# Layer 0 of a four-layer graph network: upper score blocks only, the adjacency used without a turn

## The chip, the cores and the metric

One core of one Trainium2 chip runs the whole program. The metric is the device time of one execution in microseconds (us). Engines are named as in the profile: PE is TensorE (matrix products and transposes), PEld its weight loads, DVE is VectorE, ACT is ScalarE, POOL is GpSimd, and SP is the engine that issues most DMAs.

## The reference, cut to what matters

There are 16 graphs ("batches") of 1024 nodes with 128 features. Layer 0 is a graph attention, and the change lies in it and in how its adjacency reaches layer 1.

```
h = x @ W_w.T + W_b
e = einsum('bjl,bkl->bjk', h @ A, h);  e = e + swapaxes(e, 1, 2)      # symmetric
att = where(adj > 0, e, -9e15);  att = softmax(att, axis=1) * adj
h_prime = relu(einsum('bij,bjk->bik', att, h))
coeff = sigmoid(concatenate([x, h_prime]) @ gate_w.T + gate_b)
x = layernorm(x + coeff * x + (1 - coeff) * h_prime)
```

The inputs are built as `adj = a | a.T | eye`, so each adjacency is symmetric, holds 0 and 1, and has a full diagonal. Layer 1 first thins the adjacency row by row ("dilation"), then runs three neighbour averages with weights and norms. Layer 2 is another attention and layer 3 a small graph convolution.

## The kernel before, in words

The program is one Python function `fast_kernel`. It also computes a flag from several arrays, among them `other`, `bad`, `past` and `nomem`; where the flag is set, a second function, `general_kernel`, recomputes everything. `other` is filled in layer 0 and is non-zero where an adjacency entry is neither 0 nor 1.

A batch's rows are handled in 8 tiles of 128. Layer 0 has three generators. `before(s, b)` loads the eight adjacency row tiles `an` (fp32, 512 KB each, two buffers), and for each one: ACT copies it to bf16 `ab` and sums the rows to `deg` (L922); DVE compares it with its own 0/1 form into `chk` and counts differences in `other` (L925); PE turns its eight blocks into the PSUM tile `pt` (L929); DVE writes them as fp8 columns of `Y[b]` (L930). In between, for tiles 1, 3, 5 and 7, it also forms `xT`, `hT`, `G` (the product of `As0` = A + A.T with `hT`) and `hn` (L934 to L949). At its end POOL stores `Y[b]` to memory, to `adj8_d[b]` (L951), for layers 2 and 3.

`attention(s, b)` goes over eight tiles jt: ACT makes a mask `msk` from a row tile of `Y` (0 for an edge, -2^53 for none, L962); PE computes the 128x1024 scores `e` from `hT` and `G` in two halves of 512 columns (`wide_matmul`, L723; the fp32 product is shown as two matmul records per half); DVE adds mask and scores into `em` with the row maximum as a by-product (L965) and negates it (L967); ACT takes the exponential in place (L969); DVE forms the reciprocal of the sum and scales the rows of `hn` to `hs` (L971, L973); PE adds `hs` times `em` to `acc` (L976). `after(s, b)` applies gate, sum and layer norm, and POOL stores the result to `x1_d`.

`in_turn` runs `after(b-1)`, `attention(b)` and `before(b+1)` alternately, so that batches overlap; at the end `attention(15)` runs beside `after(14)` alone. A scheduler then fixes each engine's instruction order in advance; on the chip every engine works through its own list in that order. The PSUM pools are `ps_w` (two score tiles of two banks), `ps_a` (`acc`) and `ps_h` (two tiles of one bank, shared by `pt` and all the small products).

The fp8 adjacency of all 16 batches stays on chip after layer 0, as four tiles of four batches, `Yq[0]` to `Yq[3]` ("quarters", the tiles called `carry`). Dilation works on it in two groups of eight batches (`GB` = 8): for each of eight blocks k and each group g, `prepare` forms counts, `fixed_point` finds the thresholds and `removal` clears edges. The order of (k, g) is the list `steps`. The batches 0 to 7 are stored to `dil8_d` (`dil_d` in the profile) after their last removal (L1154), and their space becomes `wide_pool` of layer 1, which holds the fp32 pieces `a` and the reloaded `A8` tiles. Layer 1 begins with batch 8.

Of the kernel before, what the change touches and what calls it, by code (L numbers as in the profile page):

```python
# [22 lines left out]
P = 128  # L23
NEG = -9000000000000000.0
BIG = 2.0 ** 53
# [4 lines left out]
QB = 4  # L30
# [609 lines left out]
def fast_kernel(ctx: ExitStack, tc: tile.TileContext, t: dict, out: bass.AP, flag: bass.AP):  # L640

    nc = tc.nc
    B, N, D = t["x"].shape
    NT = N // P
    H2 = N // 512
    BT = B * NT

    consts = ctx.enter_context(tc.tile_pool(name="consts", bufs=1))
    dram = ctx.enter_context(tc.tile_pool(name="dram", bufs=1, space=DRAM))

    identf = consts.tile([P, P], F32, name="identf")
    make_identity(nc, identf)
    identb = consts.tile([P, P], BF16, name="identb")
# [8 lines left out]
    adj8_d = [dram.tile([P, NT, N // 4], F32, name=f"adj8_d{b}") for b in range(B)]  # L662
# [9 lines left out]
    deg = consts.tile([P, BT], F32, name="deg")  # L672
# [1 line left out]

    bad = consts.tile([P, 2, NT, B], BF16, name="bad")
    past = consts.tile([P, NT - 2, B], F32, name="past")
    other = consts.tile([P, BT], F32, name="other")

    mx0 = consts.tile([P, BT], F32, name="mx0")
    zeros = mx0  # L680
# [39 lines left out]
    def wide_matmul(psum, lhsT, rhs, tag="w"):  # L720
        p = psum.tile([P, N], F32, name="pmm", tag=tag)
        for h in range(H2):
            nc.tensor.matmul(p[:, h * 512:(h + 1) * 512], lhsT, rhs[:, h * 512:(h + 1) * 512],  # L723
                             start=True, stop=True)
        return p
# [151 lines left out]


    carry_ctx, carry2_ctx = ExitStack(), ExitStack()
    Yq = []  # L880
    for ctx_, side in ((carry2_ctx, "right"), (carry_ctx, "left")):
        pool = ctx_.enter_context(tc.tile_pool(name=f"carry_{side}", bufs=1, side=side))
        Yq += [pool.tile([P, QB, NT, N], FP8, name=f"carry{len(Yq) + i}") for i in range(B // QB // 2)]
    Y = [Yq[b // QB][:, b % QB] for b in range(B)]

# [3 lines left out]
    with ExitStack() as ph:  # L889

        early = ph.enter_context(tc.tile_pool(name="l0_early", bufs=1, reuse_waits="tile"))
        wts = ph.enter_context(tc.tile_pool(name="l0_w", bufs=1, reuse_waits="tile"))
        ps_w = ph.enter_context(tc.tile_pool(name="l0_pw", bufs=2, space=PSUM, reuse_waits="tile"))
        ps_a = ph.enter_context(tc.tile_pool(name="l0_pa", bufs=1, space=PSUM, reuse_waits="tile"))
        ps_h = ph.enter_context(tc.tile_pool(name="l0_ph", bufs=2, space=PSUM, reuse_waits="tile"))

        with tc.tile_pool(name="l0_raw", bufs=1) as raw:
            W0T = transposed(wts, ps_h, matrix(raw, t["L0_gnn_W_w"], "l0W"), "l0WT", "h")
            As0 = symmetric(wts, ps_h, matrix(raw, t["L0_gnn_A"], "l0A"), "l0As", "h")
        work = ph.enter_context(tc.tile_pool(name="l0_work", bufs=1, reuse_waits="tile"))  # L900
        small = ph.enter_context(tc.tile_pool(name="l0_small", bufs=2, reuse_waits="tile"))
        b0 = column(wts, t["L0_gnn_W_b"], "l0b")
        gw = wts.tile([P, 2, 32], F32, name="l0gw")
# [4 lines left out]
        gbh = wts.tile([P, 1], F32, name="l0gbh")  # L908
        nc.vector.tensor_scalar(gbh, gb, 0.5, None, op0=OP.mult)
        nbig = wts.tile([P, 1], F32, name="l0nbig")  # L910
        nc.vector.memset(nbig, -BIG)

        def before(s, b):

            s.xn = work.tile([P, NT, P], F32, name="xn", bufs=3)
            nc.sync.dma_start(s.xn, nat(t["x"][b]))
            for it in range(NT):
                c = b * NT + it
                an = early.tile([P, N], F32, name="an", bufs=2)
                nc.sync.dma_start(an, t["adj"][b][it * P:(it + 1) * P, :])  # L920
                ab = early.tile([P, N], BF16, name="ab", bufs=2)
                nc.scalar.activation(ab, an, AF.Copy, accum_out=deg[:, c:c + 1])  # L922

                chk = early.tile([P, N], FP8, name="chk")
                nc.vector.scalar_tensor_tensor(chk, an, 0.0, an, op0=OP.is_gt, op1=OP.not_equal,  # L925
                                               accum_out=other[:, c:c + 1], saturate=False)
                pt = ps_h.tile([P, NT, P], BF16, name="pt", tag="h")
                for jt in range(NT):
                    nc.tensor.transpose(pt[:, jt, :], ab[:, jt * P:(jt + 1) * P], identb)  # L929
                nc.vector.tensor_scalar(Y[b][:, :, it * P:(it + 1) * P], pt, 0.0, None, op0=OP.is_gt, saturate=False)  # L930
                if it == 1:
                    xT = early.tile([P, N], F32, name="xT")
                    for p, c, _ in turned(ps_h, s.xn):
                        nc.scalar.copy(xT[:, c], p)  # L934
                elif it == 3:
                    s.hT = work.tile([P, N], F32, name="hT", bufs=2)
                    for p, c in products(ps_h, (W0T, xT)):
                        nc.scalar.activation(s.hT[:, c], p, AF.Identity, bias=b0)
                    pz = gates(ps_h, early.tile([P, N], FP8, name="chk").bitcast(F32), (gw[:, 0, :], xT))
                    s.gx = small.tile([P, NT], F32, name="gx")  # L940
                    nc.vector.tensor_copy(s.gx.rearrange("p (q t) -> p q t", t=2), pz[:, :, :, 0])
                elif it == 5:
                    s.G = work.tile([P, N], F32, name="G", bufs=2)
                    for p, c in products(ps_h, (As0, s.hT)):
                        nc.scalar.copy(s.G[:, c], p)
                elif it == 7:
                    s.hn = work.tile([P, N], F32, name="hn")
                    for p, c, _ in turned(ps_h, s.hT):
                        nc.vector.tensor_copy(s.hn[:, c], p)  # L949
                yield  # L950
            nc.gpsimd.dma_start(adj8_d[b], Y[b].bitcast(F32))  # L951

        def attention(s, b):


            s.acc = ps_a.tile([P, N], F32, name="acc")
            for jt in range(NT):
                js = slice(jt * P, (jt + 1) * P)
                c = b * NT + jt
                mx = mx0[:, c:c + 1]  # L960
                msk = work.tile([P, N], BF16, name="msk", bufs=2)
                nc.scalar.activation(msk, Y[b][:, jt, :], AF.Identity, scale=BIG, bias=nbig)  # L962
                e = wide_matmul(ps_w, s.hT[:, js], s.G)
                em = work.tile([P, N], F32, name="em", bufs=2)
                nc.vector.tensor_tensor_reduce(em, e, msk, 1.0, -3.0e38, op0=OP.add, op1=OP.max, accum_out=mx)  # L965
                nmx = small.tile([P, 1], F32, name="nmx")
                nc.vector.tensor_scalar(nmx, mx, -1.0, None, op0=OP.mult)  # L967
                sm = small.tile([P, 1], F32, name="sm")
                nc.scalar.activation(em, em, AF.Exp, bias=nmx, accum_out=sm)  # L969
                rs = small.tile([P, 1], F32, name="rs")  # L970
                nc.vector.reciprocal(rs, sm)  # L971
                hs = small.tile([P, P], F32, name="hs")
                nc.vector.tensor_scalar(hs, s.hn[:, js], rs, None, op0=OP.mult)  # L973
                for h in range(H2):
                    c = slice(h * 512, (h + 1) * 512)
                    nc.tensor.matmul(s.acc[:, c], hs, em[:, c], start=(jt == 0), stop=(jt == NT - 1))  # L976
                yield

        def after(s, b):
# [21 lines left out]

        in_turn(before, attention, after)

# [8 lines left out]
    with ExitStack() as ph:  # L1012
        sb = ph.enter_context(tc.tile_pool(name="dl_sb", bufs=2, reuse_waits="tile"))
        small = ph.enter_context(tc.tile_pool(name="dl_small", bufs=3, reuse_waits="tile"))
# [150 lines left out]


        G2 = B // GB
        steps = [(Batch(), k, g) for k in range(NT) for g in range(G2)]
        for s in steps[:G2]:
            for _ in prepare(*s):  # L1170
                pass

        nc.vector.tensor_scalar(mx0, mx0, -1.0e15, None, op0=OP.is_lt)
        nc.vector.tensor_reduce(nomem, mx0, AX.X, OP.max)

        nc.vector.tensor_scalar(deg, deg, 1.0, 1.0, op0=OP.add, op1=OP.max)
# [1 line left out]
        pt = ps_s.tile([BT, P], F32, name="pt", tag="s")  # L1178
# [74 lines left out]
    with ExitStack() as ph:  # L1253
        wts = ph.enter_context(tc.tile_pool(name="l1_w", bufs=1, reuse_waits="tile"))
        work = ph.enter_context(tc.tile_pool(name="l1_work", bufs=2, reuse_waits="tile"))
# [3 lines left out]
        small = ph.enter_context(tc.tile_pool(name="l1_small", bufs=2, reuse_waits="tile"))  # L1259
        ps_h = ph.enter_context(tc.tile_pool(name="l1_ph", bufs=4, space=PSUM, reuse_waits="tile"))  # L1260
# [185 lines left out]
        left = []  # L1446
# [4 lines left out]
        for l in range(3):  # L1451
# [9 lines left out]
            for i in range(B + lag[l]):  # L1461
                streams, left = left, []
# [22 lines left out]
            left = [rest]  # L1485
# [263 lines left out]
```

## Time and profile before

| what | value |
|---|---|
| time, median of 3 runs | 3006.41 us (3003.87, 3006.41, 3013.27) |
| profiled execution, first to last instruction | 2999.4 us |
| what lies around the span, against the median | 7.0 us |
| layer 0 (to the last norm of batch 15) | about 0 to 731 us |
| dilation | about 731 to 1146 us |
| layer 1 | about 1146 to 1820 us |
| layers 2 and 3 | the rest |
| PE busy, share of the span | 2738.3 us, 91% |
| DVE busy | 2327.9 us, 78% |
| ACT busy | 2028.5 us, 68% |

The page lists no time of its own for the profiled execution, only its span. "Busy" of an engine is time with at least one of its instructions running. In lines of groups, the part before the bar is source line, engine, operation, output<-inputs, shapes and count; behind it come busy us and the mean ns of one; behind the next bar the idle time of the engine just before such instructions and what ended it. A 40-digit row is the span in 40 slices of 75 us, each digit a tenth of busy.

### The profile page before, as it was taken

The page shows a single profiled execution, that of the slowest core. Times are in us where ns is not written, and L with a number is a line of the kernel's source. Part 1 is how long each engine was busy: PE and PEld are TensorE (multiplying, and loading weights), DVE is VectorE, ACT ScalarE, POOL GpSimd, SP SyncE. Part 2 cuts the span into 40 slices and gives each one's busy share as a digit, 9 for nine tenths or more (in the row PEclk, how much of TensorE's full clock was granted, in tenths as well). Part 3 has the DMA queues.
Part 4 walks back from the last instruction along what each step waited for, and adds up shares of the span by engine and source line. Part 5 has one row for each costly group of instructions (what it writes and reads, how often), then busy time and mean ns, then how long its engine had stood idle before and what let it go on. Part 6 is the DMA issues. An engine that isn't in the chain of part 4 may idle for free.

```text
span 2999.4 us, 43064 instructions
## 1 busy us (share of the span) xinstructions
PE 2738.3 (91%) x15282; PEld 1714.8 (57%) x15282; DVE 2327.9 (78%) x5990; ACT 2028.5 (68%) x3476; POOL 324.1 (11%) x295
## 2 busy tenths in 40 slices
PE   7999999996999998999999988999999999999996
PEld 3444444443566566887788874455555555555554
DVE  6898888887999995776688885766767777777765
ACT  5777787784788877666555534766766776666763
POOL 0000000003000001111122231000010001000000
PEclk9999999998999999999999997999999999999998
DMA  4344344431000024223367692111111121111000
GB/s 157 134 162 148 134 147 155 141 134 43 2 2 2 2 82 163 86 99 129 128 238 241 234 342 98 36 57 57 64 70 57 65 70 69 57 56 57 22 15 23
DMA packets 124129, 297.98 MB, mean 99 GB/s; under 512 B 12672, under 2 KB 65664, under 8 KB 116736
## 3 DMA queue, kind: packets, MB, share of 16 engines
q1 hardware_dynamic: 103440, 211.65, 20.8%
q0 software_dynamic: 20464, 83.47, 7.4%
q8 instruction: 123, 2.02, 0.3%
q14 instruction: 102, 0.84, 0.1%
HBM read 211.04 MB, written 84.02 MB: 98 GB/s over the span
## 4 chain that ended last, share of the span: by engine, by line
PE 36%; DVE 23%; issue 21%; ACT 8%; DMA 6%; POOL 5%; SPq 0%; POOLq 0%; ACTq 0%; DVEq 0%
PE ph L1545 8%; PE acc L1301 7%; PE ph L765 4%; PE acc L1621 4%; DMA an<-in_adj 4%; POOL ln_rstd L744 3%; PE pmm L723 3%; DVE ln_st L793 3%; PE ph L1405 3%; ACT xn L800 3%; PE ph L758 3%; DVE em L1607 2%; PE ph L1531 2%; ACT em L969 2%; PE acc L976 2%
## 5 line engine op out<-in xcount | busy, mean ns | idle before, releaser
L723 PE MATMUL pmm<-G,hT 128*128 128x512 f32 x1024 | 503.1, 608 | 7.6 <-DVE mx L1607 7.2
L800 ACT ACTIVATE xn<-xn,ln_nb,ln_rstd 128x128 f32<-128x128 f32 x512 | 207.3, 481 | 108.7 <-DVE ln_nb L798 108.7
L723 PEld LDWEIGHTS pmm<-G,hT 128*128 128x128 f32 x1024 | 178.2, 192 | 175.5 <-issue 140.6
L976 PE MATMUL acc<-em,hs 128*128 128x512 f32 x512 | 243.5, 598 | 16.6 <-DVE hs L973 15.0
L1301 PE MATMUL acc<-a,lo 128*128 128x512 f32 x768 | 243.4, 401 | 15.7 <-DVE lo L1268 15.7
L744 POOL TENSOR_TENSOR ln_rstd<-ln_rstd,mhalf 128x8 f32<-128x8 f32 (+1 forms) x68 | 113.6, 1671 | 1320.0 <-DVE nmx L1609 603.7
L1621 PE MATMUL acc<-em,hs 128*128 128x512 f32 x512 | 249.7, 606 | 3.5 <-DVE hs L1618 1.9
L1301 PE MATMUL acc<-a,hi 128*128 128x512 f32 x768 | 244.0, 402 | 3.7 <-ACT hi L1267 3.5
L1138 PE MATMUL s<-step,carry 128*128 128x512 bf16 (+2 forms) x1088 | 211.6, 307 | 4.1 <-DVE carry L1108 3.2
L1140 ACT ACTIVATE q<-s,negc 128x512 f16<-128x512 f32 x256 | 170.6, 697 | 58.4 <-DVE negc L1119 22.3
L922 ACT ACTIVATE ab<-an 128x1024 bf16<-128x1024 f32 x128 | 134.6, 1053 | 106.2 <-DMA an<-in_adj 79.5
L1152 ACT ACTIVATE carry<-pc,negone 128x512 fp8e4<-128x512 f32 x256 | 166.8, 699 | 37.0 <-PE pc L1151 27.7
L965 DVE CUSTOM_DVE_ANT_0 em<-pmm,msk 128x1024 f32<-128x1024 f32 x128 | 155.9, 1218 | 30.4 <-PE acc L976 26.5
L1607 DVE CUSTOM_DVE_ANT_0 em<-pmm,msk 128x1024 f32<-128x1024 f32 x128 | 155.6, 1216 | 26.1 <-PE acc L1621 21.3
L1301 PEld LDWEIGHTS acc<-a,lo 128*128 128x128 f32 x768 | 144.2, 190 | 54.9 <-DVE lo L1268 21.3
L925 DVE SCALAR_TENSOR_TENSOR chk<-an 128x1024 fp8e4<-128x1024 f32 x128 | 156.3, 1221 | 15.5 <-DMA an<-in_adj 15.4
L1301 PEld LDWEIGHTS acc<-a,hi 128*128 128x128 f32 x768 | 143.0, 190 | 37.1 <-ACT hi L1267 4.0
L1602 ACT ACTIVATE msk<-A,nbig 128x1024 bf16<-128x1024 fp8e4 x128 | 145.8, 1140 | 26.6 <-DVE mx L1607 23.4
L930 DVE TENSOR_SCALAR carry<-pt 128x1024 fp8e4<-128x1024 bf16 x128 | 155.5, 1216 | 7.0 <-PE pt L929 6.9
L976 PEld LDWEIGHTS acc<-em,hs 128*128 128x128 f32 x512 | 90.6, 190 | 113.0 <-issue 87.9
L969 ACT ACTIVATE em<-em,nmx 128x1024 f32<-128x1024 f32 x128 | 146.8, 1147 | 11.9 <-DVE nmx L967 11.5
L1405 PE MATMUL ph<-Wx,hT 128*128 128x128 f32 x768 | 151.6, 280 | 3.0 <-ACT nT L1430 1.5
(293 smaller groups left out, 6252.8 us busy)
## 6 DMA issues: line engine op xcount, KB each, us to landing
an<-in_adj SPq DMA_DIRECT2D x128, 512.0 KB, 4.1
adj_d<-carry POOLq DMA_DIRECT2D x16, 1024.0 KB, 4.9
A<-dil_d SPq DMA_DIRECT2D x16, 1024.0 KB, 6.8
rdeg<-rdeg_d SPq DMA_DIRECT2D x32, 512.0 KB, 4.1
ag_d<-ag POOLq DMA_DIRECT2D x32, 512.0 KB, 5.3
ag<-ag_d SPq DMA_DIRECT2D x32, 512.0 KB, 6.1
A<-adj_d SPq DMA_DIRECT2D x16, 1024.0 KB, 4.7
xn<-in_x SPq DMA_DIRECT2D x16, 512.0 KB, 3.9
```

The costliest lines, as they stand in the source:

```text
L723: nc.tensor.matmul(p[:, h * 512:(h + 1) * 512], lhsT, rhs[:, h * 512:(h + 1) * 512], start=True, stop=True)
L744: nc.gpsimd.tensor_tensor(r, r, mhalf[:, :n], op=OP.pow)
L800: nc.scalar.activation(r[:, k.start + i, :], r[:, k.start + i, :], AF.Identity, scale=rstd[:, i:i + 1], bias=nb[:, i:i + 1])
L969: nc.scalar.activation(em, em, AF.Exp, bias=nmx, accum_out=sm)
L976: nc.tensor.matmul(s.acc[:, c], hs, em[:, c], start=(jt == 0), stop=(jt == NT - 1))
L1138: nc.tensor.matmul(s[:, lo or 0:], y, twos if lo is None else step[:, :512 - lo], start=(j == 0), stop=(j == len(terms) - 1))
L1140: nc.scalar.activation(q[:, h * 512:(h + 1) * 512], s, AF.Abs, bias=st.negc[:, i:i + 1])
L1301: nc.tensor.matmul(acc, part[:, jt, :], pieces[h * NT // 2 + i][:, j, :], start=(jt == 0 and p == 0), stop=(jt == NT - 1 and p == 1))
L1405: nc.tensor.matmul(p[:, i * P:(i + 1) * P], x[:, j * P:(j + 1) * P], W, start=(n == 0), stop=(n == 1))
L1545: nc.tensor.matmul(p, part[:, jt, :], A[:, jt, c], start=(jt == 0 and i == 0), stop=(jt == NT - 1 and i == 1))
L1607: nc.vector.tensor_tensor_reduce(em, e, msk, 1.0, 0.0, op0=OP.add, op1=OP.max, accum_out=mx)
L1621: nc.tensor.matmul(s.acc[:, c], hs, em[:, c], start=(jt == 0), stop=(jt == NT - 1))
```

## The change

1. `before`: ACT's copy of `an` goes straight into row tile `it` of `Y[b]` as fp8. There is no `ab`, no turn of the whole tile and no column write. DVE compares the part of `an` right of the diagonal block with its own 0/1 form; for the diagonal block and the blocks left of it, PE multiplies the already stored blocks of `Y[b]` (which turns them) and DVE compares the result, in pieces of up to four blocks, with `an`. `other` gets three counts per tile and becomes bf16. `an` has three buffers.
2. `attention`: `G` carries a minus sign, so a row minimum replaces the maximum and no negation follows. For tile jt only the columns from the diagonal block on are multiplied and masked; the blocks left of it are transposes of the masked blocks `em` of earlier tiles, written by PE into the same PSUM tile. DVE reduces the two parts one after the other, the second starting from the result `first` of the first. The eight `em` tiles of a batch are kept (`l0_kept`, 32 KB a partition); the exponential goes to a new tile `ex`.
3. Quarters: to make room for `l0_kept`, batches 0 to 3 use the space of `Yq[3]` in layer 0, until batches 12 to 15 need it. After layer 0, `Yq[0]` takes the place of `l0_kept` and is loaded back from `adj8_d[0..3]` by SP.
4. Dilation takes group 1 (batches 8 to 15) before group 0 in each block.

```diff
-    other = consts.tile([P, BT], F32, name="other")
+    other = consts.tile([P, BT * 3], BF16, name="other")
+    nc.vector.memset(other, 0.0)
...
+    Yq = [None, quarter(carry2_ctx, 1, "right"), quarter(carry_ctx, 2, "left"), quarter(carry_ctx, 3, "left")]
+    Y = [Yq[b // QB or B // QB - 1][:, b % QB] for b in range(B)]
...
-                an = early.tile([P, N], F32, name="an", bufs=2)
+                an = early.tile([P, N], F32, name="an", bufs=3)
...
-                ab = early.tile([P, N], BF16, name="ab", bufs=2)
-                nc.scalar.activation(ab, an, AF.Copy, accum_out=deg[:, c:c + 1])
+                nc.scalar.activation(Y[b][:, it, :], an, AF.Copy, accum_out=deg[:, c:c + 1], saturate=False)
...
-                nc.vector.scalar_tensor_tensor(chk, an, 0.0, an, op0=OP.is_gt, op1=OP.not_equal,
-                                               accum_out=other[:, c:c + 1], saturate=False)
-                pt = ps_h.tile([P, NT, P], BF16, name="pt", tag="h")
-                for jt in range(NT):
-                    nc.tensor.transpose(pt[:, jt, :], ab[:, jt * P:(jt + 1) * P], identb)
-                nc.vector.tensor_scalar(Y[b][:, :, it * P:(it + 1) * P], pt, 0.0, None, op0=OP.is_gt, saturate=False)
+                done = (it + 1) * P
+                if done < N:
+                    nc.vector.scalar_tensor_tensor(chk[:, done:], an[:, done:], 0.0, an[:, done:], op0=OP.is_gt,
+                                                   op1=OP.not_equal, accum_out=other[:, 3 * c:3 * c + 1], saturate=False)
+                for h in range(it // 4 + 1):
+                    js = range(4 * h, min(4 * h + 4, it + 1))
+                    k = slice(js[0] * P, (js[-1] + 1) * P)
+                    pt = ps_h.tile([P, 512], F32, name="pt", tag="h")
+                    for i, jt in enumerate(js):
+                        nc.tensor.matmul(pt[:, i * P:(i + 1) * P], Y[b][:, jt, it * P:done], identb, start=True, stop=True)
+                    nc.vector.scalar_tensor_tensor(chk[:, k], pt[:, :k.stop - k.start], 0.0, an[:, k], op0=OP.is_gt,
+                                                   op1=OP.not_equal, accum_out=other[:, 3 * c + h + 1:3 * c + h + 2],
+                                                   saturate=False)
...
-                        nc.scalar.copy(s.G[:, c], p)
+                        nc.scalar.activation(s.G[:, c], p, AF.Copy, scale=-1.0)
...
-                nc.scalar.activation(msk, Y[b][:, jt, :], AF.Identity, scale=BIG, bias=nbig)
-                e = wide_matmul(ps_w, s.hT[:, js], s.G)
-                em = work.tile([P, N], F32, name="em", bufs=2)
-                nc.vector.tensor_tensor_reduce(em, e, msk, 1.0, -3.0e38, op0=OP.add, op1=OP.max, accum_out=mx)
-                nmx = small.tile([P, 1], F32, name="nmx")
-                nc.vector.tensor_scalar(nmx, mx, -1.0, None, op0=OP.mult)
+                nc.scalar.activation(msk[:, lo:], Y[b][:, jt, lo:], AF.Identity, scale=-BIG, bias=nbig)
+                e = ps_w.tile([P, N], F32, name="pe", tag="w")
+                for k in ([slice(lo, 512)] if jt < 4 else []) + [slice(max(lo, 512), N)]:
+                    nc.tensor.matmul(e[:, k], s.hT[:, js], s.G[:, k], start=True, stop=True)
+                for it in range(jt):
+                    nc.tensor.transpose(e[:, it * P:(it + 1) * P], em[it][:, js], identf)
+                em.append(kept.tile([P, N], F32, name=f"em{jt}"))
+                first = small.tile([P, 1], F32, name="first") if jt else mn
+                nc.vector.tensor_tensor_reduce(em[jt][:, lo:], e[:, lo:], msk[:, lo:], 1.0, 3.0e38, op0=OP.add, op1=OP.min,
+                                               accum_out=first)
+                if jt:
+                    nc.vector.tensor_scalar(em[jt][:, :lo], e[:, :lo], 1.0, first, op0=OP.mult, op1=OP.min, accum_out=mn)
+                ex = work.tile([P, N], F32, name="ex", bufs=2)
...
-                nc.scalar.activation(em, em, AF.Exp, bias=nmx, accum_out=sm)
+                nc.scalar.activation(ex, em[jt], AF.Exp, scale=-1.0, bias=mn, accum_out=sm)
...
+    Yq[0] = quarter(carry2_ctx, 0, "right")
+    for b in range(QB):
+        Y[b] = Yq[0][:, b]
+        nc.sync.dma_start(Y[b].bitcast(F32), adj8_d[b])
...
-        steps = [(Batch(), k, g) for k in range(NT) for g in range(G2)]
+        steps = [(Batch(), k, g) for k in range(NT) for g in reversed(range(G2))]
```

More of the change, by code (lines that the diff above doesn't have):

```diff
@@ L879, in fast_kernel, with quarter @@
     carry_ctx, carry2_ctx = ExitStack(), ExitStack()
[L880 to L884, printed above, removed]
+    def quarter(ctx_, q, side):
+        pool = ctx_.enter_context(tc.tile_pool(name=f"carry_{q}", bufs=1, side=side, reuse_waits="tile"))
+        return pool.tile([P, QB, NT, N], FP8, name=f"carry{q}")
+    Yq = [None, quarter(carry2_ctx, 1, "right"), quarter(carry_ctx, 2, "left"), quarter(carry_ctx, 3, "left")]
+    Y = [Yq[b // QB or B // QB - 1][:, b % QB] for b in range(B)]
     with ExitStack() as ph:
@@ L900, in fast_kernel @@
         work = ph.enter_context(tc.tile_pool(name="l0_work", bufs=1, reuse_waits="tile"))
+        kept = ph.enter_context(tc.tile_pool(name="l0_kept", bufs=1, side="right", reuse_waits="tile"))
         small = ph.enter_context(tc.tile_pool(name="l0_small", bufs=2, reuse_waits="tile"))
@@ L910, in fast_kernel @@
         nbig = wts.tile([P, 1], F32, name="l0nbig")
-        nc.vector.memset(nbig, -BIG)
+        nc.vector.memset(nbig, BIG)
         def before(s, b):
@@ L956, in attention @@
             s.acc = ps_a.tile([P, N], F32, name="acc")
+            em = []
             for jt in range(NT):
-                js = slice(jt * P, (jt + 1) * P)
+                lo = jt * P
+                js = slice(lo, lo + P)
                 c = b * NT + jt
-                mx = mx0[:, c:c + 1]
+                mn = mx0[:, c:c + 1]
                 msk = work.tile([P, N], BF16, name="msk", bufs=2)
-                nc.scalar.activation(msk, Y[b][:, jt, :], AF.Identity, scale=BIG, bias=nbig)
-                e = wide_matmul(ps_w, s.hT[:, js], s.G)
-                em = work.tile([P, N], F32, name="em", bufs=2)
-                nc.vector.tensor_tensor_reduce(em, e, msk, 1.0, -3.0e38, op0=OP.add, op1=OP.max, accum_out=mx)
-                nmx = small.tile([P, 1], F32, name="nmx")
-                nc.vector.tensor_scalar(nmx, mx, -1.0, None, op0=OP.mult)
+                nc.scalar.activation(msk[:, lo:], Y[b][:, jt, lo:], AF.Identity, scale=-BIG, bias=nbig)
[11 more added lines that the diff above has]
+                ex = work.tile([P, N], F32, name="ex", bufs=2)
                 sm = small.tile([P, 1], F32, name="sm")
-                nc.scalar.activation(em, em, AF.Exp, bias=nmx, accum_out=sm)
+                nc.scalar.activation(ex, em[jt], AF.Exp, scale=-1.0, bias=mn, accum_out=sm)
                 rs = small.tile([P, 1], F32, name="rs")
@@ L975, in attention @@
                     c = slice(h * 512, (h + 1) * 512)
-                    nc.tensor.matmul(s.acc[:, c], hs, em[:, c], start=(jt == 0), stop=(jt == NT - 1))
+                    nc.tensor.matmul(s.acc[:, c], hs, ex[:, c], start=(jt == 0), stop=(jt == NT - 1))
                 yield
@@ L1171, in fast_kernel @@
                 pass
-        nc.vector.tensor_scalar(mx0, mx0, -1.0e15, None, op0=OP.is_lt)
+        nc.vector.tensor_scalar(mx0, mx0, 1.0e15, None, op0=OP.is_gt)
         nc.vector.tensor_reduce(nomem, mx0, AX.X, OP.max)
```

## The prediction

> **What bounds the kernel now.** I read the page's slices first. Layer 0 is slices 1 to 9 (0 to about 731 us), and there TensorE is at 9 tenths in nearly every slice and VectorE at 8 or 9.
>
> ```profile
> PE   7999999996999998999999988999999999999996
> DVE  6898888887999995776688885766767777777765
> ACT  5777787784788877666555534766766776666763
> ```
>
> Then the table of busy time for a stretch of twelve batches in the steady part (window, length, then busy us of PE, weight loads, DVE, ACT, POOL):
>
> ```profile
> 102.70:621.28 518.58, 483.21 (x2160) 239.96 (x2159) 462.03 (x1104) 414.41 (x698) 37.23 (x36) 1.00 0.43 146
> ```
>
> Per batch that is 43.2 us, of which PE is busy 40.3, DVE 38.5, ACT 34.5. TensorE bounds the layer, idle only 2.9 us a batch; VectorE is a close second. The groups of the same stretch (96 row tiles) say what fills them:
>
> ```profile
> L723 PE MATMUL pmm<-G,hT 128*128 128x512 f32 x384 | 190.8, 609 | 0.0
> ...
> L925 DVE SCALAR_TENSOR_TENSOR chk<-an 128x1024 fp8e4<-128x1024 f32 x96 | 117.3, 1222 | 10.3 <-DMA an<-in_adj 10.2
> L965 DVE CUSTOM_DVE_ANT_0 em<-pmm,msk 128x1024 f32<-128x1024 f32 x96 | 116.9, 1218 | 21.4 <-PE acc L976 20.6 <-ACT msk L962 0.2
> L930 DVE TENSOR_SCALAR carry<-pt 128x1024 fp8e4<-128x1024 bf16 x96 | 116.7, 1215 | 0.6 <-PE pt L929 0.6
> ```
>
> The score matmul L723 never waits. Three full-width VectorE passes per tile (L925, L930, L965) make most of DVE. Last the waits of this stretch: ACT waits 57.8 us (4.8 a batch) for `an`, but PE's own waits on data are small, so that costs little now.
>
> ```profile
> ACT ab L922 <- DMA an<-in_adj: 57.8, 28, 5.0
> ...
> PE pt L929 <- ACT G L945: 17.5, 12, 2.3
> ```
>
> **What the Trainium skill says.** "VectorE: DVE Perf Modes", "Why PSUM operands drop a tier": an fp32 operand in PSUM runs at one element a cycle. The trace agrees: `hn<-ph` L949, 512 columns from PSUM, takes 0.68 us. So the new passes over PSUM are priced at that. "ScalarE: Activation LUTs", "What ACT_TABLE_LOAD costs": an activation with a pointer bias takes about 280 ns + 0.833 ns a column, 1.13 us at 1024; the trace has 1.137 for `msk` L962. "Perfetto Trace Analysis", "Matmuls": larger matmuls are more efficient. This trace does not show that for fp32: the 128-column passes of L1405 start every 0.11 us, the 512-column ones of L723 every 0.43. The timeline of layer 1 (start, length; two passes a row):
>
> ```profile
> 1247.07 0.39 PE L1405 MATMUL ph<-Wx,hT 128*128 128x128 f32 x2
> 1247.29 0.39 PE L1405 MATMUL ph<-Wr,ag 128*128 128x128 f32 x2
> 1247.51 0.39 PE L1405 MATMUL ph<-Wx,hT 128*128 128x128 f32 x2
> ```
>
> **The change, part by part** (per batch of layer 0).
>
> *TensorE.* Scores: 16 matmuls of 512 columns, two passes each at 0.43, are 13.8 us. Only blocks on and above the diagonal stay: 4608 of 8192 columns, and as cost goes with columns, 7.7. Saved 6.0. Added: 28 fp32 transposes of masked blocks; in the timeline eight L758 transposes take 1.04 us, the last 0.27 of it, so 0.11 each: 3.1. Adjacency: 64 bf16 transposes (16 in 1.06 us, the last 0.22: 0.056 each) are 3.6; 36 matmuls of fp8 blocks with the identity, priced the same, are 2.0. Saved 1.6. Net 4.5: PE 40.3 to 35.8.
>
> *VectorE.* A full pass follows the one before after 1.14 us (L925 at 674.11, L930 at 675.26): 1.07 for 1024 columns and 0.08 fixed. L925 and L930 were 16 passes, 18.3 us. Now there are 19 pieces over 8192 columns: 8.5 + 19 x 0.08 = 10.0, saved 8.3. The row reduction was 8 passes, 9.1; now 15 pieces, 8.5 + 1.2, with the second piece of 7 tiles waiting for its scalar `first`, about 0.1 each: 10.4. The 8 negations L967 go, about 1. Net 8.0: DVE 38.5 to 30.5.
>
> *ScalarE.* Masks lose 3584 columns x 0.833 ns = 3.0 us. The copy that fed `ab` writes fp8 rows of `Y` instead, at the same width, and G's negation is a scale on an existing copy: both nothing. ACT 34.5 to 31.5.
>
> *Waits.* PE is still the longest by 4 us, so the period is PE plus its idle time. There are more stops than before: transposes into `e` of tile jt wait for the reduction of tile jt-1; in the built order TensorE's matmuls of two tiles stand ahead of that, and `acc` matmuls of older tiles queue with them. 12 small PSUM tiles `pt` instead of 8 share the two `ps_h` buffers with 14 others. The trace does not show these waits. From below they cost nothing or less, as DVE and ACT are freer (idle falls to 1.5, period 37.3); from above each of the 7 tiles with transposes stalls PE 0.5 us (a third of its present wait for G, 17.5 us in 12): idle 6.4, period 42.2. I take one more us: idle 3.9, period 39.7. Saved 3.5 x 15 batches that run beside a neighbour = **53 us**.
>
> *Start.* Batch 0 alone takes 33.5 us to its first score (L723 at 33.51), gated by two `an` buffers and VectorE's two passes. Three buffers, and half the DVE work: -5, between -8 and, since `an` is now held until the transposed half is checked, +1.
>
> *Tail of layer 0.* Batch 15 has 30 us between its last adjacency (DVE L1176 at 685.64) and its last exp (716.03). PE would save 2.9 there. But POOL's `deg` power (L1177, 20.75 us) is issued at the same point and batch 14's `ln_rstd` stands behind it on POOL; in the built order DVE's `ln_nb` waits for that ahead of the reductions of tiles 6 and 7. In the run before POOL was done at 707.3, 1.6 us before it was asked; a shorter tail hits it. -2, between -5 and +3.
>
> *Hand-over to dilation.* Quarter 0 comes back from memory: four 1 MB loads on SP, which wait for the last exp and transposes of `em` (its space). Cover: from last exp (717.2) the output part of batch 15 runs to 731.6 and the preparation of two resident quarters to about 736: 19 us. Before moves 1 MB loads at 274 to 405 GB/s (1110 to 1150 us), so 4 MB needs 10 to 15 plus some 4 landing time. Hidden, between 0 and +6. SP has nothing else behind them but `dinv_d`. Dilation does the same instructions with groups 8-15 first. So stores of `dil_d` move from 1108-1127 to the last 18 us of the phase; the first widened `a` pieces wait for the four stores of quarter 0, which end about 10 us before. SP's `A8` loads wait for all eight, with the first `rdeg` load behind them: 5.9 us landing, then 2 MB. `rdeg` is wanted only after half of the first product, some 15 us in. +2, between -3 and +8. Added quarter-0 loads need no engine. One `other` memset: nothing. Later layers have the same instructions in locally other order: 0, +-8.
>
> **Sum:** -53 - 5 - 2 + 2 = -58. The profiled execution spans 2999.4 us, 7.0 under the median 3006.4 of the three runs; what lies around stays. So the span goes to 2941, the time to **2948**.
>
> **Rivals.**
> *A, full pay-out.* PE's idle share does not grow (2.9 or less), as DVE and ACT lose 8 and 3 us. Period 38.7 to 37.3: saved 68 to 89, with start and tail -7 to -13: 2931 down to 2906. For: L723 never waits. Against: more handshakes.
> *B, the adjacency feed becomes the bound.* `an` is held until ACT copied it, PE turned blocks and DVE compared. With 4.1 us landing and three buffers, eight tiles at 42.5 us need a hold of 11.8 us. Then 10 us + 5: about 2990. For: ACT already waits 57.8 us on it. Against: hold with two buffers is under 6.7 us now (10.8 a cycle less 4.1).
> *C, slower: a chain from tile to tile.* If each tile's transposes stood right behind the `acc` of the tile before, a loop would be: first reduction 0.75 (mean), second 0.62, exp 1.34, reciprocal and `hs` 0.44, `acc` 1.72, transposes 0.4, hand-overs 0.6: 5.9 us a tile, 47 a batch, +4 x 15: 3066. The built order keeps the `acc` some two to three tiles behind, so the loop has two or more times the room; it decides only if that lead shrinks to about 1.1 tiles (5.9 over 5.4).
> *D, it doesn't do what it says:* a check that always fires runs the general kernel after the fast one, which would add more than any term here. Symmetric 0/1 inputs speak against it.
>
> **Chances.** Forecast (2918 to 2975) 0.55; A 0.18; B or late losses (2975 to 3015) 0.19, of which a third within 9 us of now or above; C 0.06; D 0.02. 0.3%, 9 us, is about what a measurement of this kernel can tell from no change. Faster 0.85, same 0.06, slower 0.09. Range 2908 to 2998.
>
> **What would show it.** Right: per batch about 39.7 us with PE near 36, DVE near 30, ACT near 31; `pe<-G` 7.7 us a batch; layer 0 ends near 672. `ln_nb` waiting on POOL in the tail shows that step; a DVE wait on the quarter-0 DMA, the hand-over. Wrong: PE below 85% with waits on the first reduction (C), or on `an` (B), or dilation longer than now.

## The result, and the profile after

The changed kernel takes 3018.95 us (median of seven runs), the kernel before 3006.41: ratio 1.0042, 95% interval 1.0028 to 1.0056. The forecast was 2948. The profiled execution of the changed kernel spans 3012.4 us, 13.0 more than before. First the page's slices, as shown of before, with the granted TensorE clock (PEclk, tenths of full speed):

```profile
PE   7988889886999987999999987999999999999996
DVE  6777667767999994776688785766777777677765
ACT  6776767773788876666656534766666676676763
PEclk9999989998999998999999998999999999999998
```

Layer 0 (slices 1 to 9) still fills the same slices. VectorE fell there, ScalarE a little, but TensorE no longer holds its nines, and its clock falls under nine tenths in the sixth slice; before, it was at nine tenths or more in all nine. Twelve batches, from the start of one batch's `ln_rstd` on POOL to that of the batch twelve later (window, length, busy us of PE, weight loads, DVE, ACT, POOL, then granted clock, DMA share, GB/s):

```profile
125.92:661.77 535.85, 474.64 (x2064) 248.36 (x2064) 375.55 (x1345) 380.32 (x696) 41.55 (x36) 0.93 0.42 142
```

Per batch: 44.65 us, PE busy 39.55, idle 5.10, DVE 31.3, ACT 31.7, clock 0.93. The kernel before has 43.25, 40.33, 2.92 and clock 1.00 in the same kind of window. The waits of 100 to 622 us show what PE stops for (total us, times, longest us):

```profile
ACT carry L925 <- DMA an<-in_adj: 67.5, 43, 4.3
...
PE pe L977 <- DVE em L985: 23.0, 15, 2.6
...
DVE ln_nb L799 <- POOL ln_rstd L745: 17.8, 12, 1.5
...
PE ph L766 <- DVE chk L938: 12.3, 8, 1.7
...
PE pg L780 <- ACT r L777: 10.5, 8, 2.9
```

The waits of ACT and DVE are where most of it starts, the three of PE what comes of it. In one batch it reads like this. VectorE's timeline (start, length, instruction, and in brackets the idle time before it and its releaser):

```profile
438.83 0.18 DVE L742 TENSOR_SCALAR ln_rstd<-ln_mv 128x8 f32<-128x8 f32 x1
438.91 0.83 DVE L930 SCALAR_TENSOR_TENSOR chk<-an 128x640 fp8e4<-128x640 f32 x1
439.65 0.10 DVE L930 DVE_READ_ACCUMULATOR chk<-an 128x1 bf16 x1
441.30 0.17 DVE L799 SCALAR_TENSOR_TENSOR ln_nb<-ln_mv,ln_rstd 128x8 f32<-128x8 f32 x1 [1.55 <-POOL ln_rstd L745]
441.38 0.48 DVE L985 TENSOR_SCALAR_CACHE_REDUCE em<-pe,first 128x256 f32<-128x256 f32 x1
```

and TensorE's, beside it:

```profile
438.98 0.33 PE L979 MATMUL pe<-identf,em 128*128 128x128 f32 x1 [0.79 <-DVE first L982]
441.92 2.08 PE L977 MATMUL pe<-G,hT 128*128 128x512 f32 x2 [2.61 <-DVE em L985]
```

`ln_nb` waits 1.55 us for POOL's power. The second reduction L985 of a tile stands behind it in VectorE's list, and it frees the score buffer that the next L977 writes: PE stops for 2.61 us, just after another stop of 0.79; between the two it runs one transpose of 0.33 us. Then see what L977 costs when it does run: 2.08 us for two passes of 512 columns; two passes of that width (L766 at 447.84 us) take 1.06 us at full clock. The stretches around the stop, cut where the clock changes (same columns as above; the first number after the length is PE busy, the third from the right the clock):

```profile
437.67:441.08 3.41, 0.85 (x4) 0.14 (x1) 2.08 (x12) 1.76 (x3) 1.92 (x1) 1.00 0.00 0
441.08:444.49 3.41, 2.57 (x3) 1.17 (x4) 3.19 (x12) 2.99 (x8) 0.18 (x1) 0.50 0.26 84
444.49:447.91 3.42, 3.42 (x10) 1.93 (x9) 1.18 (x5) 3.03 (x6) 0.95 (x1) 0.50 0.70 236
447.91:451.32 3.41, 3.41 (x13) 1.88 (x13) 2.48 (x9) 2.23 (x4) 0.00 (x0) 1.00 0.43 158
```

The clock is halved for 6.8 us, and for the last 6 of them PE looks 100% busy and does half the work. So **a stop of PE can be paid twice**, once as idle time and once as busy time. In the twelve batches this comes 13 times, 71.7 us of half clock in all; PE is busy for 63 of them, so 31.5 us are lost, 2.6 us a batch. The Trainium skill describes the gate ("TensorE: Matmul & The Clock Gate", "What's actually happening"): half rate after an idle window of about 3.4 us, full rate after about as long of sustained work. The halving agrees, and so does the length, as every half-clock stretch lasts 3.41 or 6.83 us; but PE was not idle for the whole window, it was busy for 0.85 of the 3.41 us before the fall.

Where the 13 us of span lie, from the traces (before, after): to batch 0's first norm 101.83 to 82.32, **-19.5**; thirteen batches from there 562.2 to 579.5, **+17.2**; the rest of layer 0 **+2.3**, so dilation starts at the same moment in both, 731.6; dilation 0; hand-over, from its end to layer 1's first product with `lo`, **+7.8**; layer 1's products +4.0 and the rest +1.3. The 4.0 is not assigned: the unchanged layer 1 takes between 567.5 and 571.7 us in the runs below.

### The profile page after: what moved, and what is told of

Its sections match the earlier page's. It is cut to its first block, busy times and chain, and to the rows that moved or that the text cites. A ratio compares the mean times of both kernels' runs of the same rounds, so it can differ in the third digit from the quotient of the medians.

```text
span 3012.4 us, 43031 instructions
## 1 busy us (share of the span) xinstructions
PE 2717.1 (90%) x15091; PEld 1727.8 (57%) x15154; DVE 2211.6 (73%) x6311; ACT 1982.7 (66%) x3476; POOL 328.5 (11%) x295
## 4 chain that ended last, share of the span: by engine, by line
PE 38%; DVE 24%; issue 7%; POOL 4%; ACT 4%; DMA 2%; POOLq 0%; SPq 0%; DVEq 0%; ACTq 0%
PE ph L1568 8%; PE acc L1324 6%; PE ph L766 4%; PE acc L1644 4%; PE ph L1428 3%; PE s L1161 3%; POOL ln_rstd L745 3%; DVE ln_st L794 2%; DVE em L1630 2%; PE ph L1554 2%; PE ph L759 2%; DVE mid L1115 2%; ACT xn L801 2%; PE pmm L724 2%; DVE keep L1165 1%
## 5 line engine op out<-in xcount | busy, mean ns | idle before, releaser
L995 PE MATMUL acc<-ex,hs 128*128 128x512 f32 x512 | 255.5, 620 | 4.8 <-DVE hs L992 3.3
L724 PE MATMUL pmm<-G,hT 128*128 128x512 f32 x512 | 248.8, 607 | 7.2 <-DVE mx L1630 6.5
L1644 PE MATMUL acc<-em,hs 128*128 128x512 f32 x512 | 249.6, 606 | 3.9 <-DVE hs L1641 1.9
L1161 PE MATMUL s<-step,carry 128*128 128x384 bf16 (+3 forms) x1035 | 199.4, 303 | 7.0 <-DVE carry L1131 3.2
L925 ACT ACTIVATE carry<-an 128x1024 fp8e4<-128x1024 f32 x128 | 134.5, 1051 | 86.0 <-DMA an<-in_adj 85.7
L977 PE MATMUL pe<-G,hT 128*128 128x512 f32 (+3 forms) x384 | 163.5, 526 | 27.5 <-DVE em L985 27.4
L1630 DVE CUSTOM_DVE_ANT_0 em<-pmm,msk 128x1024 f32<-128x1024 f32 x128 | 156.0, 1219 | 24.2 <-PE acc L1644 20.3
L988 ACT ACTIVATE ex<-em,mx 128x1024 f32<-128x1024 f32 x128 | 146.1, 1142 | 25.1 <-DVE em L985 18.2
L1428 PE MATMUL ph<-Wr,ag 128*128 128x128 f32 x768 | 151.4, 280 | 3.1 <-DVE ag L1416 2.0
L724 PEld LDWEIGHTS pmm<-G,hT 128*128 128x128 f32 x512 | 89.8, 192 | 98.4 <-issue 67.4
L1634 ACT ACTIVATE em<-em,nmx 128x1024 f32<-128x1024 f32 x128 | 145.7, 1138 | 0.2 <-DVE nmx L1632 0.2
```

Source lines behind the costliest of these rows:

```text
L995: nc.tensor.matmul(s.acc[:, c], hs, ex[:, c], start=(jt == 0), stop=(jt == NT - 1))
L1161: nc.tensor.matmul(s[:, lo or 0:], y, twos if lo is None else step[:, :512 - lo], start=(j == 0), stop=(j == len(terms) - 1))
L1428: nc.tensor.matmul(p[:, i * P:(i + 1) * P], x[:, j * P:(j + 1) * P], W, start=(n == 0), stop=(n == 1))
L1630: nc.vector.tensor_tensor_reduce(em, e, msk, 1.0, 0.0, op0=OP.add, op1=OP.max, accum_out=mx)
```

## The experiments

The question is first which part loses. E1 and E2 do one part each, E3 and E4 take the hand-over.

**E1, the adjacency part alone**: `before` and `other` as in the changed kernel, everything else as before. Its core, against the kernel before:

```diff
-                ab = early.tile([P, N], BF16, name="ab", bufs=2)
-                nc.scalar.activation(ab, an, AF.Copy, accum_out=deg[:, c:c + 1])
+                nc.scalar.activation(Y[b][:, it, :], an, AF.Copy, accum_out=deg[:, c:c + 1], saturate=False)
```

> The kernel before with the adjacency part alone (rows used unturned, three buffers for an, DVE compares in pieces); attention, quarters and dilation as before. Layer 0 of the changed kernel has a period of 44.6 us a batch where 39.7 was forecast. Theory 1 (two stops a batch, one from each part: ACT waits for an with other work behind it, and DVE waits for POOL's ln_rstd with a reduction behind it; after each stop the granted TensorE clock is at half for some us): this part alone shows the first stop and not the second, its period is 42 to 44 us, and with an earlier start by about 15 us the time is 2970 to 3000. Rival B (the feed of an alone is the bound): period 44 or more, time 3000 to 3020. Rival C (the chain of attention tiles alone is the bound): period at most 41.5, time 2950 to 2975.

2963.93 us, ratio 0.9857 (0.9843 to 0.9871): 44 us gained. Twelve batches:

```profile
125.80:618.62 492.82, 468.52 (x1825) 217.59 (x1824) 368.45 (x1273) 417.36 (x697) 38.07 (x36) 1.00 0.46 154
```

41.07 us a batch, PE 39.04, idle 2.03, clock 1.00. It is faster than Theory 1 said and without the stop named for it (ACT waits only 14.6 us for `an`). It has the other one instead: its one reduction, L972, stands behind `ln_nb`, and PE stops once a batch, but the clock holds. The PE waits of 125 to 600 us:

```profile
PE pmm L724 <- DVE mx L972: 19.4, 12, 1.6
```

Rival B falls as stated: the feed of `an` alone does not bound anything. The numbers are those of Rival C, which E2 has to confirm.

**E2, the attention part alone.**

```diff
-                an = early.tile([P, N], F32, name="an", bufs=3)
+                an = early.tile([P, N], F32, name="an", bufs=2)
...
+                ab = early.tile([P, N], BF16, name="ab", bufs=2)
+                nc.scalar.activation(ab, an, AF.Copy, accum_out=deg[:, c:c + 1])
```

> The changed kernel with the adjacency part taken back (two buffers for an, the copy ab, the turn of the whole tile and the column write as before); upper scores, kept em tiles, quarters and reversed dilation stay. Theory 1 (one stop from each part): it has the second stop (DVE behind POOL's ln_rstd) and not the first, period 42 to 44 us; the 12 us at the hand-over to layer 1 stay, so the time is 3005 to 3035. Rival B (the feed of an alone): period about 41, time 2975 to 2995. Rival C (the chain of attention tiles alone): period 44.5 or more, time 3030 to 3050.

3004.84 us, ratio 0.9988 (0.9978 to 0.9998). 42.46 us a batch, PE 38.90, DVE 38.76, clock 1.00. The period is in Theory 1's range, but the stop named for it is not there: `ln_nb` waits at most 0.9 us for POOL. Rival C falls: alone, the chain of tiles does not stop PE (it does not wait for the first reduction at all; the longest wait for L985's counterpart is 1.1 us). VectorE is as full as PE. So each part alone gains, and both together lose: the loss is in how they meet.

**E3, the kernel before with dilation's groups reversed.**

```diff
-        steps = [(Batch(), k, g) for k in range(NT) for g in range(G2)]
+        steps = [(Batch(), k, g) for k in range(NT) for g in reversed(range(G2))]
```

> The kernel before with only the order of the groups in dilation reversed (batches 8 to 15 first in each block). Theory: the reversal alone costs the hand-over, because the stores of batches 0 to 7 are all issued in the last 16 us of dilation and the reload for layer 1 waits for them; the first product of layer 1 starts 10 to 14 us later and the time is 3016 to 3020. Rival: the 12 us come from the new placing of the quarters or from the reload of quarter 0; then this kernel takes 3004 to 3009.

3014.49 us, ratio 1.0021 (1.0013 to 1.0030), +6.7: between the two guesses, on the theory's side.

**E4, layer 0 takes batches 8 to 15 first, dilation in its old order.**

```diff
-    Yq = [None, quarter(carry2_ctx, 1, "right"), quarter(carry_ctx, 2, "left"), quarter(carry_ctx, 3, "left")]
+    Yq = [quarter(carry2_ctx, 0, "right"), quarter(carry2_ctx, 1, "right"), None, quarter(carry_ctx, 3, "left")]
...
-        in_turn(before, attention, after)
+        in_turn(*[lambda s, b, f=f: f(s, (b + B // 2) % B) for f in (before, attention, after)])
```

> The changed kernel, but layer 0 takes batches 8 to 15 before 0 to 7, quarter 2 (batches 8 to 11) is the one reloaded and lies where layer 0's other buffers were, and dilation has its old order (batches 0 to 7 first). Theory (reversed order costs the hand-over, nothing else there does): stores of batches 0 to 7 spread over 18 us again and before the end, the first product of layer 1 is back 10 to 14 us, layer 0 keeps its 44.6 us a batch; time 3004 to 3010. Rival (the placing or the reload costs it): 3015 to 3022.

3021.56 us, ratio 1.0043 (1.0027 to 1.0059): no gain, in the rival's range. The reload is issued only at 736.9 us, as SP waits until the store of layer 0's last norm (`x_d<-xn`) has landed, and PE waits for it:

```profile
PE s L1084 <- DMA carry<-adj_d: 22.5, 3, 20.6
```

So this run traded one loss for another and tells nothing on the reversal; E10 does. Layer 0 took 44.45 us a batch again.

E5 to E8 each take away one of the waits found above, in the changed kernel. Their expectations, and E9's, count a batch from the first `hpT` to the last, ends included (43.4 us in the changed kernel); in this measure E5 to E9 took 40.1, 41.2, 39.2, 41.2 and 40.6 us. The text gives twelve steady batches.

**E5, the compare reads `Y` instead of `an`**, so `an` is free earlier.

```diff
-    nc.vector.scalar_tensor_tensor(chk[:, k], pt[:, :k.stop - k.start], 0.0, an[:, k], ...
+    nc.vector.scalar_tensor_tensor(chk[:, k], pt[:, :k.stop - k.start], 0.0, Y[b][:, it, k], ...
```

> The changed kernel, but the compare of the turned blocks (L938) reads the fp8 row in Y[b] instead of an, so that an is free after ACT's copy and the compare of its right part. (Left out: an entry of the left part that fp8 rounds to 0 or 1 would no longer be counted.) E1 gained 44 us with the adjacency part alone and E2 about 3 with the attention part alone, yet both together lose: the two parts disturb each other. Theory 1 (in the joint kernel an is held too long, ACT waits for it 67.5 us in 12 batches with exponentials and r behind it, PE stops 2 to 3 us and runs at half clock after it): ACT's wait for an falls under 25 us, the mean granted clock of 100 to 622 us rises from 0.93 to 0.96 or more, a batch (hpT to hpT) takes 40.5 to 42 us instead of 43.4, time 2970 to 3000. Rival C (chain of attention tiles; an is only late because everything is): no change, 3012 to 3025.

2984.21 us, ratio 0.9917 (0.9900 to 0.9934), in range. A batch 40.91 us, PE 37.35, idle 3.56, clock 1.00. Of the changed kernel's SP queue, the one that issues the loads of `an`, and of E5's ACT:

```profile
SPq L924 <- DVE chk L938: 452.5, 101, 10.5
```

```profile
ACT carry L925 <- DMA an<-in_adj: 30.1, 34, 2.0
```

In the changed kernel SP waits for the last compare L938 before it may load the next `an`. In E5 it waits for the other compare, L930, instead (388.0 us), and ACT's wait falls from 67.5 to 30.1 us, not quite under the 25 expected. Rival C falls here too.

**E6, four `an` buffers**, with the last `em` tile of a batch placed in `ex`.

```diff
-                an = early.tile([P, N], F32, name="an", bufs=3)
+                an = early.tile([P, N], F32, name="an", bufs=4)
...
-                em.append(kept.tile([P, N], F32, name=f"em{jt}"))
+                em.append(kept.tile([P, N], F32, name=f"em{jt}") if jt < NT - 1 else ex)
```

> The changed kernel with four buffers for an instead of three (room for it by letting the last em tile of a batch, which is never transposed, lie in ex). Theory 1 (an held too long): like E5, a batch 40.5 to 42 us, time 2970 to 3000. If E5 gains and this doesn't, what helps in E5 is not the release of an. Rival C: 3012 to 3025.

2992.49 us, ratio 0.9939 (0.9924 to 0.9954), in range. A batch takes 41.87 us at clock 0.95. ACT's wait for `an` only falls to 53.7 us. Its stop at L985 is still 2.6 us long, and its reload of quarter 0 is issued at 701.8, 15 us after the last `hpT` instead of 5 before it, so that PE waits 16.6 us for it. `l0_kept` is 4 KB smaller here than the quarter that takes its place, which must then lie partly on other buffers; that this delays it is read from the issue time.

**E7, `ln_nb` one attention tile later.**

```diff
             rstd = power_mhalf(small, mv[:, :, 1], add=LN_EPS, name="ln_rstd")
+            yield
             nb = small.tile([P, NT], F32, name="ln_nb")
```

> The changed kernel with a yield between POOL's power and DVE's ln_nb in layer 0, so that ln_nb stands behind the work of one more attention tile on DVE. Theory 1 (the second stop: ln_nb waits 1.5 us for POOL with a second reduction behind it, which frees the PSUM tile that PE waits for, 2.6 us, then half clock): ln_nb's wait goes to nearly 0, PE's wait for L985 falls from 23 us under 12, a batch takes 41 to 42.5 us, time 2975 to 3005. Rival C: PE waits for L985 as before, 3012 to 3025.

2956.95 us, ratio 0.9828 (0.9814 to 0.9842): 62 us under the changed kernel, more than expected. A batch takes **39.69** us, PE 36.48, idle 3.21, clock 1.00. `ln_nb` still waits 8.0 us in all, at most 0.7. PE's total wait for L985 hardly changed, where a fall under 12 us was expected; its longest did change:

```profile
PE pe L977 <- DVE em L985: 21.0, 23, 1.0
```

**E8, `ln_nb` on POOL.**

```diff
-            nc.vector.scalar_tensor_tensor(nb[:, :n], mv[:, :n, 0], -1.0, rstd, op0=OP.mult, op1=OP.mult)
+            nc.vector.tensor_scalar(nm[:, :n], mv[:, :n, 0], -1.0, None, op0=OP.mult)
+            nc.gpsimd.tensor_tensor(nb[:, :n], nm[:, :n], rstd, op=OP.mult)
```

> The changed kernel with ln_nb computed on POOL (DVE negates the mean before, POOL multiplies after its power), so that DVE never waits for POOL and ACT waits for it instead. Theory 1: PE's wait for L985 falls as in E7, but ACT holds exponentials behind the norm for a longer time; a batch 41 to 43.4 us, time 2980 to 3018. Rival C: 3012 to 3025.

2985.23 us, ratio 0.9919 (0.9906 to 0.9933), in range. Twelve batches:

```profile
128.03:633.77 505.74, 446.12 (x2055) 233.61 (x2055) 371.64 (x1339) 373.32 (x694) 40.65 (x48) 1.00 0.45 150
```

This row is worth a second look: 42.15 us a batch, idle 4.97, almost the changed kernel's 5.10, but the clock is 1.00 and PE busy 37.2 instead of 39.55. Its longest stop on any wait is 2.1 us, and the clock was halved once, for 3.4 us. **The sum of idle time does not set the clock; how it is bunched does.**

A weakness remains: each of E5 to E8 also gave the scheduler another problem, and the traces show VectorE's instructions of layer 0 in another order in all four. Perhaps any other order would have been better.

**E9, POOL multiplies where it raised to a power.** This leaves the order of PE, DVE and ACT untouched; in the traces each runs the same instructions in the same order as in the changed kernel up to 640 us.

```diff
-            rstd = power_mhalf(small, mv[:, :n, 1], add=LN_EPS, name="ln_rstd")
+            rstd = power_mhalf(small, mv[:, :n, 1], add=LN_EPS, name="ln_rstd", op=op)   # OP.mult in layer 0
```

> The changed kernel with POOL multiplying instead of raising to a power in layer 0's norm (left out: the power, so the normed values differ; nothing later depends on them in time). The built order of PE, DVE and ACT is the changed kernel's, instruction for instruction; in E5 to E8 it was not. Theory 1 (stops and the half clock after them): if POOL's instruction gets at least 1 us shorter, the stop of PE at L985 (up to 2.6 us, once a batch) shrinks with it, the half-clock stretch behind that stop goes, and a batch falls from 43.4 us by 1.5 to 3.5, more than POOL's own saving; time 2965 to 2997. Rival D (any other order helps; the stops named do not matter): 3012 to 3025. If the multiplication takes as long as the power, the run tells nothing.

2986.21 us, ratio 0.9928 (0.9908 to 0.9949), 33 us under the changed kernel. POOL's instruction (shortest/median/longest ns) in the changed kernel and in E9, then E9's twelve batches:

```profile
L745 POOL TENSOR_TENSOR ln_rstd<-ln_rstd,mhalf x12: 1662/2100/2102, 125.9 to 615.8; 128x8 f32<-128x8 f32 x12
```

```profile
L745 POOL TENSOR_TENSOR ln_rstd<-ln_rstd,mhalf x12: 196/635/637, 126.8 to 583.9; 128x8 f32<-128x8 f32 x12
```

```profile
126.85:627.68 500.83, 452.93 (x2064) 237.98 (x2064) 375.07 (x1345) 378.50 (x696) 23.72 (x37) 0.98 0.45 152
```

POOL saves 1.47 us a batch, `ln_nb` no longer waits, and the batch falls by **2.9** us, from 44.65 to 41.74: 1.1 in idle time, 1.8 in PE busy time with the same instructions in the same order. The half-clock time of twelve batches falls from 71.7 to 17.1 us, and what PE loses to it from 31.5 to 8.5 us, which is 1.9 a batch. Rival D falls, and the doubling is shown directly. ACT's wait for `an` (66.7 us) and PE's for `r` (10.8, longest 3.3) stay as they were, and with them some of the lost clock (0.98).

**E10, the changed kernel with dilation's old group order.**

```diff
-        steps = [(Batch(), k, g) for k in range(NT) for g in reversed(range(G2))]
+        steps = [(Batch(), k, g) for k in range(NT) for g in range(G2)]
```

> The changed kernel with dilation's old group order (batches 0 to 7 first). Quarter 0 had landed at 728 us in the changed kernel, before the 731.6 at which dilation starts, so the reload stays hidden. Theory (the reversal costs the hand-over): the stores of batches 0 to 7 spread again, layer 1's first product comes 8 to 13 us earlier; time 3006 to 3012. Rival (the hand-over loss has another cause, or the reload is exposed as in E4): 3015 to 3022.

3012.18 us, ratio 1.0014 (1.0006 to 1.0023), against 1.0042 of the changed kernel: 8 us back, the time just above its range. The first product with `lo` comes 6 us earlier, less than the 8 to 13 expected. The stores and the first product with `lo`, of the changed kernel and then of E10 (first and last start):

```profile
L1177 POOL DMA_DIRECT2D dil_d<-carry x8: 532/532/566, 1130.3 to 1146.4; - x8
...
L1324 PEld LDWEIGHTS acc<-a,lo x768: 186/188/338, 1164.0 to 1735.5; 128*128 128x128 f32 x192
```

```profile
L1177 POOL DMA_DIRECT2D dil_d<-carry x8: 532/532/568, 1108.3 to 1126.5; - x8
...
L1324 PEld LDWEIGHTS acc<-a,lo x768: 186/188/333, 1157.7 to 1728.6; 128*128 128x128 f32 x192
```

From the start of dilation's last ReLU piece to that product it takes 18.5 us in the changed kernel and 18.1 in E3, both reversed; 12.5 here and 10.7 before. What the product waits for in the changed kernel is ACT's first rounding `hi` of the node features, and ACT waits for their load; the waits of 1135 to 1172 us and the transfers of 1138 to 1160 (the last number is us from issue to landing):

```profile
ACT hi L1290 <- DMA n<-x_d: 8.1, 1, 8.1
```

```profile
dil_d<-carry POOLq DMA_DIRECT2D x4, 1024.0 KB, 9.3
A<-dil_d SPq DMA_DIRECT2D x2, 1024.0 KB, 5.9
n<-x_d SPq DMA_DIRECT2D x3, 512.0 KB, 13.4
```

The late stores are under way together with these loads, which land in 13.4 us here and 13.2 in E3, but in 7.5 in E10 and 4.2 before. That the stores are what slows them is read from this; no run changed the loads alone. The reload of quarter 0 is not quite hidden when group 0 goes first: PE waits 4.1 us for it in E10.

**E11, both edits together**: E7's `yield` and E10's line.

> E7 (ln_nb behind one more attention tile) with dilation's old group order. Theory: both gains add, layer 0 at 39.2 us a batch and the hand-over back: 2944 to 2951. Rival (reversal costs nothing): 2954 to 2960.

**2945.82 us**, ratio 0.9796 (0.9776 to 0.9815), the fastest of all and ahead of both kernels: 61 us under the kernel before. Twelve batches take 39.78 us each, PE 36.52, idle 3.26:

```profile
124.67:602.06 477.39, 438.27 (x2065) 236.46 (x2065) 379.52 (x1345) 377.86 (x696) 43.38 (x36) 1.00 0.46 159
```

**E12, E11 with E6's edit as well**: four `an` buffers, the last `em` tile in `ex`.

> E11 with four buffers for an as in E6. In E7 ACT still waits 28.6 us for an in 12 batches, but PE idles only 3.2 us a batch, mostly for the score buffer (L985). Theory 1: most of that wait is covered, so a batch falls by 0 to 0.7 us, time 2934 to 2951. If an is still what stops PE: by over 0.7, under 2934.

2957.20 us, ratio 0.9835 (0.9816 to 0.9854), slower than E11 and than expected. The batch did fall, to 39.42 us, as expected; but as in E6 the reload comes late, and now group 0, which needs it, goes first:

```profile
PE s L1096 <- DMA carry<-adj_d: 23.2, 4, 16.6
```

## Why the prediction was wrong

**The step that failed is "Waits".** It said "the period is PE plus its idle time" with PE at 35.8, gave idle a value of 3.9 and bounds of 1.5 to 6.4. The idle time, 5.10, fell inside these bounds; the period, 44.65, did not fall inside 37.3 to 42.2. PE's busy time itself grew with the stops. E11 does the same work at full clock in 36.52 us a batch. So of the 4.95 us between 39.7 and 44.65, **2.6 are half clock** by the clock record, 1.2 more idle time and 0.7 work that was priced too low; 0.4 of PE's busy time is not assigned. Bounds on idle time alone could not hold the cost of a stop. With the stops short, E7 and E11 take 39.69 and 39.78 us a batch. That this meets the forecast's number so well is luck: their idle time is 0.6 to 0.7 below the forecast's and their work 0.7 above.

**TensorE's work**: 35.8 forecast, 36.5 at full clock (E11). **VectorE**: 30.5 forecast, 31.3 measured. **ScalarE**: 31.5 against 31.7. These three sums held.

**Which stops.** The prediction listed the first reduction, the transposes and the `pt` buffers. These did come: in four of the twelve batches PE waits 1.1 to 1.7 us for a `pt` buffer (L938) and then 1.1 to 1.2 us for the first reduction, which stands behind `ln_nb`, and the clock halves each time. The longest stops were two others: the second reduction behind `ln_nb` (2.61 us, in four other batches; in the last four it waits 1.71 us behind the norm's statistics), and `r` on ACT behind the wait for `an` (2.88 us). The first of them was in sight: the tail step names "`ln_nb` waits for that ahead of the reductions of tiles 6 and 7", and `ln_nb` waited in the kernel before too (9.4 us in 100 to 622 us), but there PE waited for no score buffer behind it. The change put the reductions that free it there. The second reduction alone is not the reason: E1 has only one, and it stands there too. E9 gives the wait for POOL's power 2.9 us of the 5.0. How the other 2 us split between the hold of `an` and the order built around it stays open, since E5 and E6 changed the order as well, and E7 cut ACT's wait for `an` to 28.6 us without touching its buffers.

**Start**: -5 forecast (-8 to +1), -19.5 measured to batch 0's first norm. 10.7 of it is batch 0's own adjacency (its store to `adj8_d` starts at 30.2 instead of 40.8 us); the start comes mostly from the adjacency part, as E1 has its first norm at 84.8 and E2 at 96.3. **Tail**: -2 forecast, +2.3, within its bounds; POOL was done 2.1 us before `ln_rstd` was asked of it, so the stop named there did not come. **Hand-over**: the reload was hidden, as said (landed by 728, wanted at 731.6). The stores were priced at +2 with bounds of -3 to +8; E3, E10 and E11 against E7 put the reversal at 7 to 11 us, at and over the edge. The step looked at `A8` and `rdeg`, which were covered, and not at the loads of `n` (512 KB each) that run together with the late stores. **Dilation and later layers**: 0 and +5, within the 8. **Around the span**: the 7.0 us are not a fixed cost. In every recorded execution that has both, the time is 1.7 to 2.0 us above the span, so the rest is that the profiled execution was a fast one. The difference of the two kernels is not touched by this.

**The rivals.** A's PE share did not come. B was half right: `an` is held until L938 (SP's wait of 452.5 us), but as a bound by itself it is refuted by E1. That it hurts together with the attention part rests on E5 and E6, which changed the order as well. C named the wrong chain: PE waited 7.6 us in twelve batches on the first reduction, which stood behind `ln_nb` in the longest of these waits, and E2 shows no loss from it. What turned the sign was none of the four: stops of known causes, many of them paid twice.

## What to carry to other kernels

Price a stop of a nearly full TensorE at its idle time plus the half clock that can come behind it, and judge a schedule by TensorE's emptiest few us, not by the sum of its idle time: 5.0 us idle a batch cost 0.1 us of half clock in E8 and 2.6 in the changed kernel. When a change alters the order, look at what stands ahead of each instruction that frees a buffer; a wait that was harmless becomes a stop once a buffer hangs behind it. And measure the halves of a change apart: here one half alone was worth 44 us, and the whole less than nothing until one instruction was moved.

## What the runs showed of the hardware

- The granted clock was 1.00 or 0.50, and it changed only on a fixed grid of time: in every trace the changes lie whole multiples of 3.41 us apart. What counted was how long PE was busy in the grid's stretch just before. In the 14 traces, from 100 to 640 us, the clock fell 66 times, each time after a stretch with PE busy for at most 51% of it. Of the stretches that it did not fall after, one lay at 43% (in E10), all others at 49% or more. A second stretch at half clock followed where PE was busy for up to 81% of the first, none from 86% on. Below, E9, where two stops of 0.70 and 1.15 us were enough, and E1, which stays just above the limit about once a batch:

```profile
416.19:419.60 3.41, 1.56 (x5) 0.54 (x4) 3.33 (x19) 2.70 (x6) 0.64 (x1) 1.00 0.00 1
419.60:423.02 3.42, 3.42 (x8) 1.74 (x7) 2.41 (x8) 3.42 (x9) 0.88 (x1) 0.50 0.47 153
```

```profile
209.40:212.81 3.41, 1.78 (x5) 0.87 (x5) 2.85 (x10) 3.03 (x9) 0.18 (x1) 1.00 0.43 143
212.81:216.22 3.41, 3.41 (x9) 1.52 (x8) 1.63 (x5) 3.34 (x6) 0.95 (x1) 1.00 0.77 237
```

  So where a stop lies on the grid matters as well as its length. One of the four stops of 2.61 us (at 575.93) left PE busy for 49% of its stretch, and the clock held; in the kernel before, PE stopped for up to 2.3 us (`pt` behind G, 1.5 on average) once a batch, and the clock fell once in twelve batches. That the limit is about half is read from these traces; no run was made to find it. The Trainium skill's rule in "HAM oscillation — how this bites in real kernels", no idle gaps over about 3.4 us, is too lax for this trace.
- POOL's power on 128x8 values mostly takes 1.66 us in the kernel before, E1 and E2 and 2.10 in the changed kernel, a multiplication of the same shape 0.20 in E8 and mostly 0.635 in E9. What adds the 0.44 us is open.
